# The head of a two-FFN attention kernel: constant matmuls ahead of the data, ternary weights by quarters, one block normalized on ScalarE

## The chip, the cores and the metric

The kernel runs on one core of a Trainium2 chip. The core has five engines that run side by side, each through its own instructions in order: TensorE (PE in the profile, PEld its weight loads), VectorE (DVE), ScalarE (ACT), GpSimd (POOL) and SyncE (SP, which here only issues transfers). They wait for each other through semaphores. The metric is the device time of one execution in microseconds, the median over several runs.

## The reference

The input x is 16 sequences of 256 tokens of 256 features, in fp32: 4096 rows of 256. Three stages each add to it:

```
x = x + 0.5 * ffn(layernorm(x))
x = x + attention(layernorm(x))          # 16 heads of 16, rotary, causal, softmax
x = x + 0.5 * ffn(layernorm(x))          # the same ffn weights

ffn(h) = gelu(h @ q(w1).T + b1) @ q(w2).T + b2
q(w)   = clip(round(w / mean(|w|)), -1, 1)
```

w1 is 1024 x 256 and w2 is 256 x 1024. So before the first FFN matmul can run, the mean of the absolute values of all of w1 has to be known, and before the second, that of w2. The rounded values are -1, 0 and 1: an element is 1 where it is over half the mean, and -1 where it is under minus half the mean.

## The kernel before

The rows are held in SBUF in 8 blocks of 512 tokens (`xs`), 4 groups of 128 partitions each. The two FFN stages run block by block; the attention stage runs sequence by sequence and is staggered with them. Only the head of the first FFN stage is touched here.

The order of the work on each engine is the order in which the program's lines issue it: the wrapper `InOrder` (lines 159 to 174) keeps every operation of an engine in program order. All these operations carry the wrapper's line, L167, in the profile, and are told apart by the tiles they write and read.

Loading. SP and ScalarE issue the transfers: block 0 of x, w1, b1, w2, b2, then the other seven blocks of x, then the attention weights. GpSimd meanwhile fills constants, among them `averaging` (128 x 128, line 119).

`begin` (line 352) does the head of the FFN. `measure` takes the layer-norm statistics of the block's four groups on VectorE (`stats`, two instructions for each group, line 178), and `finish_stats` turns four variances into reciprocal standard deviations (`rstd`) on GpSimd, in two instructions. `sizes` (line 208) sums the absolute values of a weight matrix, one part on VectorE and the rest on ScalarE for w1, both parts on ScalarE for w2. `prepare` normalizes the four groups (`xn`). `threshold` (line 221) lets TensorE sum over partitions by a matmul with `averaging`, and VectorE writes plus and minus half the mean (`half`). `signs` (line 232) makes the ternary values of a part of a matrix with two VectorE instructions: "smaller than minus half" into the result, then "greater than plus half, minus what is there". `turn_in` transposes one half of the normalized features with four TensorE transposes, ScalarE casts the result to the rounded matmul type (`xnT`, the high part), and VectorE subtracts to get the rest, so that a value goes through TensorE as a high part and a rest.

`step(u)` (line 366) is one of 64 steps and two late ones; i is the block and f one of 8 slices of 128 hidden features. In it `up` (line 301) does four matmuls of 512 columns into a PSUM tile `m` (2 buffers), ScalarE computes the gelu twice (`h_high`, rounded, and `h_whole`), and VectorE, or GpSimd for f = 1, 3, 5, subtracts (`h_rest`). `down` (line 322) does the eight matmuls of the slice two steps earlier with w2's ternary values (`w2q`). An up uses the slice f of w1's ternary values (`w1q`), a down the slice f of w2q.

In the first block the steps also carry, in this order after the up: threshold and signs of the first half of w2 at step 0, signs of the second half at step 3, statistics of block 1 at step 1, of block 2 at steps 4 to 7, the normalization of block 1 at step 3 on VectorE, its two turn_in at steps 5 and 6, and on GpSimd the halving of b2 at step 4 and its addition to x at step 6. Both halves of w1 are made in `begin`, one before and one after the transposes of block 0.

Of the kernel before, what the change touches and what calls it, by code (L numbers as in the profile page):

```python
# [8 lines left out]
FP = mybir.dt.float32  # L9
FR = mybir.dt.float32r  # L10
AF = mybir.ActivationFunctionType
ALU = mybir.AluOpType
# [17 lines left out]
def kernel(  # L30
# [144 lines left out]
    def tokens(n):  # L175
        return xs[n // BT][:, n % BT, :]
# [14 lines left out]
        )  # L191

    def normalize(ln, n, to, engine=None):
        (engine or vector).tensor_scalar(
            to,
            tokens(n),
            mv[ln][:, n, 0:1],
            rstd[ln][:, n : n + 1],
            ALU.subtract,
            ALU.mult,  # L200
        )
# [6 lines left out]
    def sizes(n):  # L208
        for k in range(2):
            part = (flat1, flat2)[n][:, k * FF : (k + 1) * FF]  # L210
            total = totals[n][:, k : k + 1]
            if n == 0 and k == 0:
                vector.tensor_reduce(total, part, AX.X, ALU.add, apply_absolute_value=True)
            else:

                size = w2q[:, k * NFC // 2 : (k + 1) * NFC // 2, :]
                scalar.activation(
                    size.rearrange("p k d -> p (k d)"), part, AF.Abs, accum_out=total
                )

    def threshold(n):
        mean = ps_mm.tile([P, 1], FP, name="mm")
# [9 lines left out]
    def signs(n, of):  # L232

        w, to = of((w1, w2)[n]), of((w1q, w2q)[n])
        vector.tensor_scalar(to, w, half[n][:, 1:2], None, ALU.is_lt)
        vector.scalar_tensor_tensor(
            to, w, half[n][:, 0:1], to.bitcast(FP), ALU.is_gt, ALU.subtract
        )
# [34 lines left out]
    def ffn(ln, after):  # L273
        xn, xnT, hT, ys = {}, {}, {}, {}

        def measure(i):
            if ln == 0:
                for t in range(BT):
                    stats(0, i * BT + t)
                finish_stats(0, i * BT, BT)  # L280
# [20 lines left out]
        def up(i, f):  # L301
            h = ps_m.tile([P, TB], FP, name="m")
            for n in range(2):
                for k in range(KC):
                    tensor.matmul(
                        h,
                        w1q[:, k, f * P : (f + 1) * P],
                        xnT[i][n][:, k, :],
                        start=(n == 0 and k == 0),
                        stop=(n == 1 and k == KC - 1),  # L310
                    )
            high = fp.tile([P, TB], FR, name="h_high", bufs=LATE + 3)
            rest = fp.tile([P, TB], FR, name="h_rest", bufs=LATE + 3)
            whole = fp.tile([P, TB], FP, name="h_whole", bufs=3)
            scalar.activation(high, h, AF.Gelu, bias=b1_sb[:, f : f + 1])
            scalar.activation(whole, h, AF.Gelu, bias=b1_sb[:, f : f + 1])

            engine = gpsimd if f in (1, 3, 5) and not (ln == 0 and i == NBLK - 1) else vector
            engine.tensor_sub(rest, whole, high.bitcast(FP))
            hT[i, f] = (high, rest)  # L320

        def down(i, f):
# [20 lines left out]
            if f == NFC - 1:  # L343
# [5 lines left out]
                for t in range(0, BT, 2):  # L349
                    after(i, t)  # L350

        def begin():
            measure(0)
            if ln == 0:
                sizes(0)
            prepare(0)
            if ln == 0:
                threshold(0)
                signs(0, lambda w: w[:, :, 0 : FF // 2])
            for k in range(KC):  # L360
                turn_in(0, k)()
            if ln == 0:
                signs(0, lambda w: w[:, :, FF // 2 :])
                sizes(1)

        def step(u):
            i, f = divmod(u, NFC)
            if i < NBLK:
                up(i, f)
                if ln == 0 and u == 0:  # L370
                    threshold(1)
                if ln == 0 and u in (0, 3):
                    part = slice(0, NFC // 2) if u == 0 else slice(NFC // 2, NFC)
                    signs(1, lambda w: w[:, part, :])
                if ln == 0 and u == 4:
                    gpsimd.tensor_scalar(b2_sb, b2_sb, 0.5, 0.0, ALU.mult, ALU.add)
                if u == 1:
                    measure(1)
                if ln == 0 and f >= 4 and i + 2 < NBLK:
                    stats(0, (i + 2) * BT + f - 4)  # L380
                    if f == NFC - 1:
                        finish_stats(0, (i + 2) * BT, BT)
                if i + 1 < NBLK:
                    if f == 3:
                        prepare(i + 1)
                    if f in (5, 6):
                        turn_in(i + 1, f - 5)()
                if f == (1 if i == NBLK - 1 else 6):
                    add_bias(i)
            if u >= LATE:  # L390
                down(*divmod(u - LATE, NFC))
            if ln == 0 and u == 2 * NFC + 2:
                make_tables()
            if ln == 0 and u < (NBLK - 1) * NFC and later:
                later.pop(0)()
# [425 lines left out]
```

## Time and profile before

| | us |
|---|---|
| median of 3 runs | 626.92 (625.38 to 626.99) |
| the profiled execution | 622.22 |
| its span | 620.4 |
| TensorE busy | 599.5 (97%) |
| VectorE busy | 461.2 (74%) |
| ScalarE busy | 416.3 (67%) |
| GpSimd busy | 300.9 (49%) |

The span is what the profiler saw from the first to the last instruction; the execution's own time lies 1.8 us above it. Busy time counts an engine's instructions; matmuls overlap, and their ends are modelled, so a busy TensorE may still be a slow one. In a timeline row the first number is the start in us from the span's start, the second the time that the merged instructions took from the first start to the last end; then the engine, the operation, the tiles written and read, shapes and count. "idle before" in square brackets names what ended the engine's wait. An fp32 matmul shows as two records, one in the rounded type as one. The engine table of the page reads, by slices of the span, that TensorE is busy nine tenths and more in all but the first slice and one later.

### The profile page before, as it was taken

What the parts mean: (1) busy time and instruction counts of PE and PEld (TensorE: products, weight loads), DVE (VectorE), ACT (ScalarE), POOL (GpSimd) and SP (SyncE); (2) the same over time, 40 slices, a digit from 0 to 9 for tenths busy, and PEclk for the clock granted to TensorE, in tenths of its full rate; (3) what the DMA queues carried; (4) which work ended last, traced back from release to release, by engine and by line L of the source; (5) the groups of instructions that cost most, each with busy time, mean ns of one, the idle gap of its engine ahead of it and who ended that gap; (6) DMA issues with size and microseconds to landing.
All of it is one profiled execution on the core that took longest, in us unless ns stands there. A gap on an engine that the chain in (4) does not pass through costs nothing.

```text
span 620.4 us, 14716 instructions
## 1 busy us (share of the span) xinstructions
PE 599.5 (97%) x5580; PEld 486.6 (78%) x5580; DVE 461.2 (74%) x1654; ACT 416.3 (67%) x716; POOL 300.9 (49%) x273
## 2 busy tenths in 40 slices
PE   4999999999999999999999999999998999999997
PEld 3798999887667777777777777777766798888886
DVE  6877777786788888888888888888886465555553
ACT  4666766664576677676777677767765676676674
POOL 3655555782464455545564456453430243334443
PEclk9999999999999999999999999999999999999999
DMA  8800000000001000100001000100100011011001
GB/s 285 180 22 1 2 1 18 17 1 18 20 35 38 19 21 36 38 27 29 19 36 38 20 20 36 37 20 21 36 4 2 1 35 35 34 35 35 27 21 55
DMA packets 25478, 21.30 MB, mean 34 GB/s; under 512 B 10944, under 2 KB 21056, under 8 KB 25408
## 3 DMA queue, kind: packets, MB, share of 16 engines
q1 hardware_dynamic: 24848, 19.44, 9.8%
q8 instruction: 44, 0.72, 0.5%
q10 hardware_dynamic: 560, 0.92, 0.4%
q14 instruction: 26, 0.21, 0.1%
HBM read 7.51 MB, written 4.19 MB: 19 GB/s over the span
## 4 chain that ended last, share of the span: by engine, by line
PE 89%; DVE 5%; ACT 3%; issue 1%; DMA 1%; POOL 1%; DVEq 0%; SPq 0%; POOLq 0%
PE mm L167 38%; PE w L167 29%; PE m L167 22%; DMA w<-in_w1T_dram 1%; DVE h_rest L167 1%; DVE xn L167 1%; ACT h_high L167 1%; ACT h_whole L167 1%; DVE w2q L167 1%; DVE st L167 1%; DVE w L167 0%; DVE x L167 0%; DVE masked L167 0%; DVE mv L167 0%; ACT pT L167 0%
## 5 line engine op out<-in xcount | busy, mean ns | idle before, releaser
L167 DVE CUSTOM_DVE_ANT_0 masked<-m,mask_q 128x128 f32<-128x128 f32 x480 | 142.7, 354 | 41.0 <-PE m L167 39.7
L167 PE MATMUL m<-xnT,w1q 128*128 128x512 f32 x512 | 145.1, 404 | 0.8 <-ACT xnT L167 0.7
L167 ACT ACTIVATE h_high<-m,b_sb 128x512 fp32r<-128x512 f32 x128 | 88.5, 691 | 78.2 <-PE m L167 78.1
L167 DVE TENSOR_TENSOR h_rest<-h_whole,h_high 128x512 fp32r<-128x512 f32 x83 | 75.0, 904 | 72.0 <-ACT h_whole L167 71.5
L167 ACT ACTIVATE pT<-w 128x768 f32<-128x768 f32 x128 | 104.1, 815 | 31.4 <-DVE w L167 24.9
L167 PE MATMUL w<-qT,kT 32*128 32x256 f32 (+1 forms) x1024 | 120.6, 348 | 1.9 <-ACT pT L167 1.8
L167 PE MATMUL w<-w2q,h_high 128*128 128x256 f32 x480 | 120.8, 285 | 0.7 <-DVE w2q L167 0.7
L167 PE MATMUL w<-w2q,h_rest 128*128 128x256 f32 x480 | 117.8, 279 | 0.4 <-POOL h_rest L167 0.3
L167 PEld LDWEIGHTS w<-qT,kT 32*128 32x128 f32 x1024 | 89.9, 184 | 33.0 <-issue 25.9
L167 PE MATMUL m<-kT,qT 32*128 32x128 f32 x960 | 114.9, 349 | 0.7 <-ACT kT L167 0.7
L167 POOL TENSOR_TENSOR h_rest<-h_whole,h_high 128x512 fp32r<-128x512 f32 x45 | 60.1, 1335 | 108.5 <-ACT h_whole L167 108.4
L167 PEld LDWEIGHTS m<-xnT,w1q 128*128 128x128 f32 x512 | 88.3, 190 | 16.7 <-DVE xnT L167 2.9
L167 PEld LDWEIGHTS w<-w2q,h_rest 128*128 128x128 f32 x480 | 90.4, 188 | 5.1 <-POOL h_rest L167 0.7
L167 PEld LDWEIGHTS w<-w2q,h_high 128*128 128x128 f32 x480 | 90.3, 188 | 5.2 <-DVE w2q L167 1.2
L167 DVE TENSOR_TENSOR w<-w,mask_k 128x512 f32<-128x512 f32 x128 | 88.8, 695 | 7.1 <-PE w L167 7.0
L167 ACT ACTIVATE h_whole<-m,b_sb 128x512 f32<-128x512 f32 x128 | 87.3, 682 | 0.0
L167 PEld LDWEIGHTS m<-kT,qT 32*128 32x128 f32 x960 | 65.9, 185 | 2.9 <-ACT kT L167 1.6
L167 POOL TENSOR_TENSOR w<-w,cosT 128x512 f32<-128x512 f32 x32 | 41.3, 1292 | 51.8 <-ACT w L167 31.9
L167 PE MATMUL mm<-xnT_a,wqk 128*128 128x256 f32 x256 | 62.2, 386 | 0.0
L167 POOL TENSOR_SCALAR var<-mv 128x4 f32<-128x4 f32 (+1 forms) x32 | 6.9, 216 | 106.2 <-DVE mv L167 105.6
L167 POOL TENSOR_TENSOR w<-w,sinT 128x512 f32<-128x512 f32 x32 | 41.0, 1280 | 26.0 <-DMA w<-w 25.9
L167 PEld LDWEIGHTS mm<-xnT_a,wqk 128*128 128x128 f32 x256 | 46.1, 190 | 7.6 <-issue 0.7
(86 smaller groups left out, 918.9 us busy)
## 6 DMA issues: line engine op xcount, KB each, us to landing
w<-w SPq DMA_DIRECT2D x64, 128.0 KB
out_dram<-x SPq DMA_DIRECT2D x15, 256.0 KB
x<-in_x_dram SPq DMA_DIRECT2D x7, 512.0 KB
w<-in_w2T_dram SPq DMA_DIRECT2D x1, 1024.0 KB
qT<-mT SPq DMA_DIRECT2D x64, 4.0 KB
w<-in_w1T_dram SPq DMA_DIRECT2D x1, 512.0 KB
w<-in_w1T_dram ACTq DMA_DIRECT2D x1, 512.0 KB
wqk<-in_wqkvT_dram SPq DMA_DIRECT2D x16, 32.0 KB
```

The costliest lines, as they stand in the source:

```text
L167: return tc.keep_in_program_order(getattr(self.engine, name)(*args, **kwargs))
```

## The change

Three things are changed, all in the head of the first FFN stage.

- `turn_on(n)` issues n matmuls of the constant tile with itself into a PSUM tile that nobody reads: 20 after the statistics of block 0 are issued, before TensorE's threshold of w1, and 4 after the transposes of block 0.
- The ternary values are made by quarters (two slices f of a matrix), not by halves. Quarter 0 of w1 comes before the transposes of block 0, quarter 1 after them; quarters 2 and 3 at steps 2 and 3. The threshold and quarter 0 of w2 are issued within `up` of step 0, between its gelu and its subtraction; quarter 1 at step 1, quarters 2 and 3 at steps 4 and 5.
- Block 1: its statistics are taken one group a step at steps 1 to 4, instead of all four at step 1, and finished at step 4. Its normalization goes from VectorE at step 3 to ScalarE at step 5, as `rstd * x - mean * rstd`; VectorE prepares the product `less` in one 128 x 1 instruction for each group. Its turn_in move from steps 5 and 6 to steps 6 and 7.

```diff
     def normalize(ln, n, to, engine=None):
+        if engine is scalar:
+            less = small.tile([P, 1], FP, name="less")
+            vector.scalar_tensor_tensor(
+                less, mv[ln][:, n, 0:1], -1.0, rstd[ln][:, n : n + 1], ALU.mult, ALU.mult
+            )
+            scalar.activation(
+                to, tokens(n), AF.Identity, bias=less, scale=rstd[ln][:, n : n + 1]
+            )
+            return
...
+    def turn_on(n):
+
+        on = ps_m.tile([P, P], FP, name="m")
+        for _ in range(n):
+            tensor.matmul(on, averaging, averaging, start=True, stop=True)
...
             scalar.activation(whole, h, AF.Gelu, bias=b1_sb[:, f : f + 1])
+            if ln == 0 and (i, f) == (0, 0):
+                threshold(1)
+                signs(1, quarter(1, 0))
...
+        def quarter(n, k):
+
+            at = slice(2 * k * P, 2 * (k + 1) * P) if n == 0 else slice(2 * k, 2 * (k + 1))
+            return (lambda w: w[:, :, at]) if n == 0 else (lambda w: w[:, at, :])
+
         def begin():
             measure(0)
             if ln == 0:
+                turn_on(20)
                 sizes(0)
             prepare(0)
             if ln == 0:
                 threshold(0)
-                signs(0, lambda w: w[:, :, 0 : FF // 2])
+                signs(0, quarter(0, 0))
             for k in range(KC):
                 turn_in(0, k)()
             if ln == 0:
-                signs(0, lambda w: w[:, :, FF // 2 :])
+                turn_on(4)
+                signs(0, quarter(0, 1))
                 sizes(1)
...
                 up(i, f)
-                if ln == 0 and u == 0:
-                    threshold(1)
-                if ln == 0 and u in (0, 3):
-                    part = slice(0, NFC // 2) if u == 0 else slice(NFC // 2, NFC)
-                    signs(1, lambda w: w[:, part, :])
+
+                soon = {1: (1, 1), 2: (0, 2), 3: (0, 3), 4: (1, 2), 5: (1, 3)}
+                if ln == 0 and u in soon:
+                    signs(soon[u][0], quarter(*soon[u]))
                 if ln == 0 and u == 4:
                     gpsimd.tensor_scalar(b2_sb, b2_sb, 0.5, 0.0, ALU.mult, ALU.add)
-                if u == 1:
-                    measure(1)
+                if ln == 0 and 1 <= u <= BT:
+                    stats(0, BT + u - 1)
+                    if u == BT:
+                        finish_stats(0, BT, BT)
...
-                    if f == 3:
-                        prepare(i + 1)
-                    if f in (5, 6):
-                        turn_in(i + 1, f - 5)()
+
+                    late = 2 if ln == 0 and i == 0 else 0
+                    if f == 3 + late:
+                        prepare(i + 1, scalar if late else None)
+                    if f in (5 + late // 2, 6 + late // 2):
+                        turn_in(i + 1, f - 5 - late // 2)()
```

## The prediction

> **What bounds the kernel now.** First the page: its chain that ended last says which engine sets the end.
>
> ```profile
> PE 89%; DVE 5%; ACT 3%; issue 1%; DMA 1%; POOL 1%; DVEq 0%; SPq 0%; POOLq 0%
> ```
>
> TensorE (PE) sets it, so a change is worth what it moves PE. All edits lie before the second block's first matmul, so second I read PE's timeline there.
>
> ```profile
> 8.22 0.98 PE L167 MATMUL mm<-totals,averaging 128*128 128x1 f32 x4 [8.22 <-DVE totals L167]
> 11.75 2.05 PE L167 MATMUL m<-xnT,w1q 128*128 128x512 f32 x4 [0.74 <-ACT xnT L167]
> 14.30 3.08 PE L167 MATMUL m<-xnT,w1q 128*128 128x512 f32 x8
> ...
> 27.30 0.60 PE L167 MATMUL mm<-ident,xn 128*128 128x128 f32 x4
> 27.65 0.36 PE L167 MATMUL w<-w2q,h_high 128*128 128x256 f32 x1
> ...
> 28.67 1.09 PE L167 MATMUL m<-xnT,w1q 128*128 128x512 f32 x4
> 29.60 0.28 PE L167 MATMUL w<-w2q,h_high 128*128 128x256 f32 x1
> ...
> 30.54 1.09 PE L167 MATMUL m<-xnT,w1q 128*128 128x512 f32 x4
> 31.47 0.28 PE L167 MATMUL w<-w2q,h_high 128*128 128x256 f32 x1
> ```
>
> From 27.65 on there is no gap: an up is 0.93 us (28.67 to 29.60), a down 0.94 (29.60 to 30.54), four transposes 0.35 (27.30 to 27.65). The second block starts at 30.54 and its first up is over at 31.47. From 11.75 the same work without gaps (8 ups, 6 downs, 2 x 4 transposes) would take 13.8 us, not 18.8: 5.0 us of slow matmuls and waits are there to be won. At full speed an up ends 1.09 after its start and ScalarE follows at 1.13; the ups at 11.75 and 14.30 took nearly twice that, though the granted clock in the rows of all windows is 1.00.
>
> Third, what the other engines did there (VectorE is DVE, GpSimd POOL):
>
> ```profile
> 9.53 0.75 DVE L167 TENSOR_SCALAR w1q<-w,half 128x1024 fp32r<-128x1024 f32 x1
> 10.32 1.28 DVE L167 SCALAR_TENSOR_TENSOR w1q<-w,half,w1q 128x1024 fp32r<-128x1024 f32 x1
> 11.52 1.28 DVE L167 TENSOR_TENSOR xnT<-mm,xnT 128x512 fp32r<-128x512 f32 x2
> ...
> 15.74 0.22 DVE L167 TENSOR_SCALAR half<-mm 128x1 f32<-128x1 f32 x2
> ...
> 21.49 1.28 DVE L167 SCALAR_TENSOR_TENSOR w2q<-w,half,w2q 128x1024 fp32r<-128x1024 f32 x1
> 22.69 2.52 DVE L167 TENSOR_SCALAR xn<-x,mv,rstd 128x256 f32<-128x256 f32 x4
> 25.13 0.68 DVE L167 TENSOR_TENSOR h_rest<-h_whole,h_high 128x512 fp32r<-128x512 f32 x1
> ```
> ```profile
> 22.29 1.64 POOL L167 TENSOR_TENSOR h_rest<-h_whole,h_high 128x512 fp32r<-128x512 f32 x1
> ```
> ```profile
> L167 ACT ACTIVATE kT<-w,one,own 128x256 f32<-128x256 f32 x64 | 38.1, 595 | 0.0
> ```
>
> DVE hardly rests from 8 to 27 us: it is the limit of this stretch. And DVE and POOL get in each other's way: the four normalizations at 22.69 took 2.52 us, against 1.37 for the same four at 7.99, because POOL's subtraction of 22.29 ran to 23.93 first; PE's first transpose of them starts at 24.23.
>
> **The change, part by part.** *Quarters.* A half costs 0.79 + 1.20 from start to start (9.53, 10.32, 11.52). A quarter's first instruction lies between the 256-wide normalization (0.32) and 0.75: by the line through them 0.48, 0.52 to the dependent next. The second costs like a 512-wide subtraction, 0.61 start to start. A quarter is 1.14, eight cost 9.1 against 8.0 for four halves: +1.1 us on DVE. Ends: 1.00 (half a half) and 1.22 (0.08 more).
>
> *The second block.* Its four DVE normalizations (2.5 us) go. ScalarE gets four of the kind of the kT row (per-partition scale and bias): 0.49 apart, 2.0 in all (ends: 0.40, the qT row's distance, and 0.59, kT's own duration), all of it on the path, since ScalarE is in order behind the sixth gelu pair and in front of the seventh. DVE gets four 128x1 instructions, 0.07 to 0.11 each as for the halves' thresholds: 0.3. They wait for rstd, with DVE's step-6 subtraction queued behind them, ScalarE's seventh gelu pair and both casts behind the normalizations, and on PE all downs from the fifth on behind the transposes. And rstd for the fourth statistic, which moves from behind the first w2 half to between the third w2 quarter and the next block's statistic. Transposes move one step later (steps 6 and 7), so only a down and one up stand between the last ones and the second block.
>
> *The 24 constant matmuls.* An fp32 matmul shows as two records. Cold, a record is 0.21 (the transposes at 9.06) to 0.245 (four in 0.98); warm, 0.09 (transposes) to 0.12 (half of a 256-wide fp32 record, 0.24). The first 20 can start at 1.1, after POOL's memset of the constants, and must be over by 8.22. All 40 records cold end at 9.6 to 10.9; warm from the start at 4.7 to 5.9. PE went fast at about 16.5 after an unbroken run from 13.17, 3.4 us: so I take 15 cold and 25 warm records, end at 7.6, cost nothing; the cover is the wait for the first weights, and beyond it every us delays the threshold and all of DVE's chain. The later four fill about 9.9 to 10.85, where the first up waits for weights anyway.
>
> *The new order, followed.* Threshold 9.27 as before (DVE's own normalizations end there). First quarter to 10.67, two subtractions to 11.89, second quarter to 13.03. PE, fast, has the transposes done at 9.9, ScalarE's casts end 10.97 (before 11.63), its two size sums 13.15 (before 13.72), so the w2 threshold reaches DVE at 13.55 instead of 15.74. That is the gain: 2.2 us. From there DVE must do, before the four small instructions: thresholds 0.25, six quarters 6.84, three subtractions 1.83, six statistics of 0.56 (4 of this block, 2 of the next), 3.36: together 12.3 us. Before, the same place needed 15.74 to 25.2 for thresholds, two halves, one subtraction, four statistics and the normalizations.
>
> Without any wait, the small instructions start at 25.85 and the normalized block is ready at 28.1, three microseconds later than the 25.2 of before. Two waits come on top. POOL's subtraction of step 1 becomes due at 16.05, among quarters, and that of step 3 at about 19.0; each holds DVE for 1.17 (such a row of POOL, 38.61 to 40.04, begins to work at 38.87, when DVE's third of four normalizations from 37.86 is over by 0.34 each), less what DVE can do meanwhile: statistics run beside POOL unhurt (0.39 to 0.42 at 17.98 to 20.0). And the subtraction of step 4 waits 0.3 for its gelu, since its up needs the third w1 quarter. With both POOL turns in full the third w1 quarter is ready at 21.35 (fifth up 21.45, before 21.04), the fourth statistic at 26.2, rstd at 27.5, hidden behind DVE's last quarter; small instructions 28.46, xn ready 30.5, transposes over at T = 30.65. If POOL's turns fall partly beside statistics, T = 29.25.
>
> From T: down 0.94, up 0.93, ScalarE's gelu pair ends at T + 3.25, cast T + 3.83; DVE in order does a subtraction (from T + 3.4), a statistic, then the transposed rest to T + 5.2; PE's first up of block two ends at T + 5.6. Before, 31.47. So T = 30.65 gives +4.8, T = 29.25 gives +3.4, no POOL wait (T = 28.2) +2.3. The unseen prices add ends of -1.2 (6 x 0.14 and 0.36) and +0.9 (6 x 0.08 and 0.4). I take +4.8: POOL asks within 0.05 us of the end of a DVE instruction, and in the row of 22.29 the waiting POOL went first.
>
> *Hidden edits.* The constants' results are read by nobody, so their buffers hold up only PE itself. SP's queue and its DMAs are unchanged; the second block's x is read from about 17 instead of 17.98, and the 3.1 MB up to its end are moved by about 12 (the windows of 2 us from 2 to 12 show 302, 404, 360, 278 and 214 GB/s). GpSimd's halving of b2 now runs before the rstd pair and costs 0.4 of POOL, idle then. Without that idleness it would delay rstd by 0.4. After 31.47 PE is without gaps and everything follows by the same shift.
>
> The sum: the profiled execution took 622.22 (span 620.4), so 622.2 + 4.8 = 627.0; the median of the runs shown is 626.92, 4.7 above that execution, and I carry the shift over: **631.7 us**.
>
> A rule that speaks against the change: the Trainium skill, "TensorE: Matmul & The Clock Gate", section "HAM oscillation — how this bites in real kernels", warns of idle gaps over about 3.4 us, after which the array falls back to half clock. By that page alone the sum would be an estimated 1.7 us higher (half of one 3.4 us window). No row here shows PE falling back.
>
> **Rivals.**
> 1. *PE goes slow again.* With T = 30.65 PE's seventh up ends at 26.1, and PE sits 4.4 us. For: the slow ups at the start. Against: no gap that long exists later in this trace. Bounds: nothing, to one down, two ups and transposes at half speed, 0.94 + 2 x 0.92 + 0.5 = 3.3. Total +6.5 as a middle, +8.1 at most: 633.4 to 635.0.
> 2. *The first 20 run too long.* All cold ends at 9.6 to 10.9, 1.4 to 2.7 behind 8.22: +6.2 to +7.5, 633.1 to 634.4. Against: the 3.4 us of 13.17 to 16.5.
> 3. *POOL finds its turns beside statistics.* +2.3, 629.2; decided by whether its two subtractions start inside statistics.
> 4. *Faster.* DVE's chain of 12.3 us is cheaper. Break-even needs T = 25.9, so small instructions at 23.6: 10.1 us without any POOL wait, that is quarters at 0.77 instead of 1.14. Below that the gain of the early threshold survives, 0.6 us for each 0.1; at 0.40 it is -2.1, 624.8. Against: the instruction rows above; a fixed part of 0.2 per instruction is not halved.
> 5. *No effect:* a longer wait at the second block but shorter ones behind it. For this PE would need gaps just behind 31.47; it has none to 40.
>
> **How the numbers follow.** The forecast, +3.4 to +4.8, 0.52; rival 1, 0.20; rival 2, 0.08; rival 3, 0.09 (half of it slower by over 0.3%, as 2.3 us is 0.37%); rival 4, 0.06 (all counted as faster); rival 5, 0.05. 0.3%, about 1.9 us, is what a measurement can tell from no change. Slower 0.52 + 0.20 + 0.08 + 0.05 = 0.85, same 0.04 + 0.05 = 0.09, faster 0.06. The range runs from just under rival 3 to rival 1's upper part: 628.8 to 634.8, which leaves out rivals 4 and 5 and the extremes of 1 and 2.
>
> **What would show it.** Right: fast first ups (about 1.1 us, not 2.05); w2's threshold on DVE near 13.5; quarter pairs near 1.14; POOL's subtractions between quarters; the ScalarE normalizations starting near 28.5; a PE gap of about 4 us before the transposes; second block's first up over near 36. Wrong: those normalizations starting before 24, or the 20 matmuls ending after 8.3.

## The result and the profile after

The changed kernel takes 634.59 us (median of 6 runs, 631.73 to 637.81), the kernel before 626.75 (6 runs, 622.22 to 626.99): 7.8 us more. The ratio on record is 1.0167, 95% interval 1.0138 to 1.0195; that is more than the quotient of these two medians (1.0125), and how it was formed is not recorded. Of 626.75 it is 10.5 us. The kernel is slower, as forecast, but by 7.8 to 10.5 us instead of 4.8. The profiled execution took 634.47 us (span 632.7). Some profiled executions have stretches of half TensorE clock late in the kernel (after 150 us) and some have none; of the other executions only the mean granted clock is known, and the lower it is, the longer they took. Before's profiled execution, without any such stretch, took 622.2; after's shortest run, whose granted clock of 0.995 is what the head's stretches alone give (6.8 us at half clock, read below, are 0.5% of 632), took 631.73. So at an equal late clock the change costs 9.5 us, and that is what has to be explained.

The page of after first, its chain that ended last:

```profile
PE 87%; DVE 6%; ACT 3%; issue 1%; POOL 1%; DVEq 0%; POOLq 0%
```

PE's share fell from 89 to 87%, DVE's rose. Then PE's timeline from the start to the second block (start, duration, instruction, the wait before it in brackets):

```profile
11.01 1.61 PE L167 MATMUL m<-xnT,w1q 128*128 128x512 f32 x4
...
13.30 2.11 PE L167 MATMUL m<-xnT,w1q 128*128 128x512 f32 x8
...
21.12 1.17 PE L167 MATMUL m<-xnT,w1q 128*128 128x512 f32 x4 [2.43 <-DVE w1q L167]
...
23.46 1.91 PE L167 MATMUL m<-xnT,w1q 128*128 128x512 f32 x4
...
29.57 0.33 PE L167 MATMUL mm<-ident,xn 128*128 128x128 f32 x1 [2.00 <-ACT xn L167]
...
31.88 0.33 PE L167 MATMUL mm<-ident,xn 128*128 128x128 f32 x1 [1.48 <-ACT xn L167]
...
32.45 0.36 PE L167 MATMUL w<-w2q,h_high 128*128 128x256 f32 x1
...
34.01 1.91 PE L167 MATMUL m<-xnT,w1q 128*128 128x512 f32 x4
...
39.13 0.50 PE L167 MATMUL m<-xnT,w1q 128*128 128x512 f32 x1 [0.65 <-DVE xnT L167]
39.47 0.28 PE L167 MATMUL w<-w2q,h_high 128*128 128x256 f32 x1
```

The early ups are faster, as meant: the first takes 1.61 us, against 2.05, the next two 2.11 together, against 3.08. The fifth up waits 2.43 us for its quarter of w1. The down behind the transposes, forecast at T = 30.65, starts at 32.45. And the second block's first up, over at 31.47 before, is over at 39.47 (call this time the mark): +8.0 us, of which the forecast had 4.8. Two ups, at 23.46 and 34.01, take 1.91 instead of 1.09.

DVE's and POOL's timelines tell why:

```profile
13.48 0.22 DVE L167 TENSOR_SCALAR half<-mm 128x1 f32<-128x1 f32 x2 [0.24 <-PE mm L167]
13.80 0.49 DVE L167 TENSOR_SCALAR w2q<-w,half 128x512 fp32r<-128x512 f32 x1
14.32 0.75 DVE L167 SCALAR_TENSOR_TENSOR w2q<-w,half,w2q 128x512 fp32r<-128x512 f32 x1
...
19.35 1.63 DVE L167 SCALAR_TENSOR_TENSOR w1q<-w,half,w1q 128x512 fp32r<-128x512 f32 x1
...
28.22 3.04 DVE L167 SCALAR_TENSOR_TENSOR less<-mv,rstd 128x1 f32<-128x1 f32 x4
```
```profile
19.12 1.30 POOL L167 TENSOR_TENSOR h_rest<-h_whole,h_high 128x512 fp32r<-128x512 f32 x1 [1.90 <-ACT h_whole L167]
...
28.83 2.34 POOL L167 TENSOR_TENSOR x<-x,b_sb 128x1024 f32<-128x1024 f32 x1
```

w2's threshold comes at 13.48, a quarter's second instruction takes 0.75 and 1.63 beside POOL's subtraction, the four small instructions start at 28.22: all close to the forecast. But these four, 128x1 each, take 3.04 us, across POOL's addition of b2 (28.83 to 31.17). ScalarE's timeline shows the same break, two normalizations before the end of that addition and two after it:

```profile
28.92 1.09 ACT L167 ACTIVATE xn<-x,less,rstd 128x256 f32<-128x256 f32 x2 [2.25 <-DVE less L167]
31.23 1.09 ACT L167 ACTIVATE xn<-x,less,rstd 128x256 f32<-128x256 f32 x2 [1.21 <-DVE less L167]
```

And the table of windows shows the clock (window, its length, busy time of PE, PEld, DVE, ACT, POOL, then the granted PE clock):

```profile
20.00:22.00 2.00, 0.88 (x4) 0.77 (x5) 1.93 (x5) 0.00 (x0) 1.16 (x2) 1.00 1.17 315
22.00:24.00 2.00, 2.00 (x12) 1.86 (x11) 1.58 (x4) 1.27 (x2) 0.00 (x0) 0.64 0.71 71
24.00:26.00 2.00, 2.00 (x8) 1.71 (x7) 1.93 (x6) 0.59 (x2) 0.00 (x0) 0.50 0.37 38
...
32.00:34.00 2.00, 1.84 (x10) 1.65 (x11) 0.50 (x1) 1.94 (x4) 0.00 (x0) 0.70 0.56 143
34.00:36.00 2.00, 2.00 (x7) 1.51 (x7) 1.28 (x4) 0.04 (x1) 0.00 (x0) 0.50 0.00 0
```

PE fell to half clock twice: (1 - 0.64) x 2 x 2 = 1.4 us of the window from 22 and all 2.0 of the next, 3.4 us; the same again from about 32.8. (Near the start such rows read 1.00 although PE is slow there: the 40 records of constants from 1.12 on take 6.81 us, while 32 of the same kind take 3.73 in the run below that keeps the clock. The rows show a fall, not the slow beginning.) Each stretch follows a time in which PE had little to do.

### The profile page after: what moved, and what is told of

The parts are those of the page before. It is cut to its first block, busy times and chain, and to the rows that moved or that the text cites. A ratio compares the mean times of both kernels' runs of the same rounds, so it can differ in the third digit from the quotient of the medians.

```text
span 632.7 us, 14827 instructions
## 1 busy us (share of the span) xinstructions
PE 613.3 (97%) x5628; PEld 497.8 (79%) x5628; DVE 464.5 (73%) x1662; ACT 417.6 (66%) x720; POOL 299.9 (47%) x273
## 4 chain that ended last, share of the span: by engine, by line
PE 87%; DVE 6%; ACT 3%; issue 1%; POOL 1%; DVEq 0%; POOLq 0%
PE mm L167 37%; PE w L167 28%; PE m L167 22%; DVE h_rest L167 1%; DVE w2q L167 1%; ACT h_high L167 1%; ACT h_whole L167 1%; DVE st L167 1%; DVE xn L167 1%; DVE less L167 0%; DVE w L167 0%; DVE x L167 0%; DVE masked L167 0%; DVE w1q L167 0%; DVE mv L167 0%
## 5 line engine op out<-in xcount | busy, mean ns | idle before, releaser
L167 PE MATMUL w<-w2q,h_high 128*128 128x256 f32 x480 | 123.0, 288 | 0.0
L167 PE MATMUL w<-w2q,h_rest 128*128 128x256 f32 x480 | 120.8, 284 | 0.5 <-POOL h_rest L167 0.2
L167 PEld LDWEIGHTS w<-w2q,h_high 128*128 128x128 f32 x480 | 91.7, 191 | 4.4 <-issue 0.3
```

Of the source, the lines that this page charges most:

```text
L167: return tc.keep_in_program_order(getattr(self.engine, name)(*args, **kwargs))
```

## The experiments

The theory at the start (A): the head is longer because the second block's statistics and normalization now stand behind all of DVE's quarters; on top come what POOL holds up and the half clock. The rivals: it is the quarters, the constants, or the ScalarE normalization as such, in whatever place.

### The three parts alone

**Constants only** (before, with the constants):

```diff
             if ln == 0:
+                turn_on(20)
                 sizes(0)
...
             if ln == 0:
+                turn_on(4)
                 signs(0, lambda w: w[:, :, FF // 2 :])
```

> The kernel before with the 24 constant matmuls alone. Mark: the end of the second block's first up, 31.47 us in the kernel before, 39.47 in the changed one. Theory A (VectorE's chain sets the head, the changed kernel is late because of the order of VectorE's work): the first ups are fast, but the first down still waits for the w2 half that VectorE finishes near 18.1, so the mark stays at 31.5 (within 0.3) and the time is the same. Theory C (TensorE's clock is what matters): the mark comes 1 to 2 us earlier.

Measured: 625.15 us against 624.7, ratio 1.0007 (0.9976 to 1.0038). PE's first ups are fast, and the time goes to the wait behind them. PE stood still all of 16 to 18 in the profiled execution, and then fell to half clock (the table of windows of this run):

```profile
16.00:18.00 2.00, 0.00 (x0) 0.00 (x0) 1.96 (x2) 1.25 (x3) 1.32 (x1) 1.00 1.10 347
18.00:20.00 2.00, 1.39 (x9) 1.39 (x10) 1.90 (x7) 0.00 (x0) 0.00 (x0) 0.82 1.11 350
20.00:22.00 2.00, 2.00 (x7) 1.61 (x7) 1.93 (x6) 0.10 (x1) 1.13 (x2) 0.50 1.16 323
```

The mark was at 33.14, 1.6 us behind the 31.5 that A expected; half of 3.4 us at half clock is 1.7. C, which expected it 1 to 2 us earlier, does not hold. The runs at a granted clock of 1.000 took 622.6 to 622.7, 0.2 to 0.6 more than before's at 0.998 to 1.000 beside them (622.1 to 622.4): alone the constants give nothing.

**Quarters only** (before, with the quarters and their places):

```diff
-                signs(0, lambda w: w[:, :, 0 : FF // 2])
+                signs(0, quarter(0, 0))
...
+                soon = {1: (1, 1), 2: (0, 2), 3: (0, 3), 4: (1, 2), 5: (1, 3)}
+                if ln == 0 and u in soon:
+                    signs(soon[u][0], quarter(*soon[u]))
```

> The kernel before with the quarters alone, in the changed kernel's order; second block as before (statistics at step 1, VectorE normalization at step 3), no constants. A: 1.1 us more VectorE work, and w1's last two quarters now stand ahead of the normalization: mark near 33 (+1.5). Theory B (what costs is the second block's new place and engine, the quarters are free): mark 31.5.

Measured: 626.84 us, ratio 1.0049 (1.0026 to 1.0072), mark 34.70, 1.7 us behind what A expected. The fifth up waits 3.11 us for its quarter, and 3.4 us of half clock follow here too. So in this order the quarters are not free.

**Second block only** (before, with its later statistics, its ScalarE normalization and its later transposes):

```diff
-                if u == 1:
-                    measure(1)
+                if ln == 0 and 1 <= u <= BT:
+                    stats(0, BT + u - 1)
+                    if u == BT:
+                        finish_stats(0, BT, BT)
...
+                    late = 2 if ln == 0 and i == 0 else 0
+                    if f == 3 + late:
+                        prepare(i + 1, scalar if late else None)
```

> The kernel before with the second block's edits alone (one statistic a step, ScalarE normalization at step 5, turn-in at steps 6 and 7), halves, no constants. A: rstd comes after the fourth statistic at about 25 to 26, GpSimd's addition of b2 may hold the four small instructions for 2 us: mark 35 to 37 (+4 to +5.5). B: the whole of the +8.0, mark 39 or later.

Measured: 630.37 us, ratio 1.011 (1.0072 to 1.0149), mark 38.35, between what A and B expected: this part alone puts the mark 6.9 us back. PE waits from 26.0 to 28.1 and again for 1.34 us before the third transpose, because POOL's addition (2.35 us) cuts the four small instructions in two here as well (3.58 us for the four). The windows from 28 to 34 have a clock of 0.50. The three marks (+1.7, +3.2 and +6.9) do not add up to the +8.0: each part alone draws half clock of its own.

### Is it the addition of b2, is it the clock?

**Bias late** (the changed kernel, the first block's addition of b2 two steps later):

```diff
-                if f == (1 if i == NBLK - 1 else 6):
+                if f == (1 if i == NBLK - 1 else 6) and not (ln == 0 and i == 0):
                     add_bias(i)
+                if ln == 0 and u == NFC:
+                    add_bias(0)
```

> The changed kernel with GpSimd's addition of b2 to block 0 moved from step 6 to step 8. A: the four small instructions take 0.3 us instead of 3.04, the normalized block comes 1.9 us earlier, mark 37.5 or, if TensorE then also keeps its clock, 36. B: it is the late rstd alone, mark stays at 39.5.

Measured once: 630.91 us. The small instructions take 0.88 us instead of 3.04, DVE's timeline:

```profile
29.09 0.88 DVE L167 SCALAR_TENSOR_TENSOR less<-mv,rstd 128x1 f32<-128x1 f32 x4
```

That the addition held them is shown. The mark still came at 39.03, for in this execution the first half clock fell on the fifth up itself (1.96 us from 21.22) and put everything behind it 0.9 us back; the second began at about 31.6.

**Clock kept** (the changed kernel, with more constants in PE's two gaps):

```diff
             if i < NBLK:
+                if ln == 0 and u == 4:
+                    turn_on(8)
                 up(i, f)
+                if ln == 0 and u == 6:
+                    turn_on(16)
```

> The changed kernel with 8 more constant matmuls ahead of the fifth up and 16 ahead of the second block's first transposes, where TensorE stood idle for 2.4 and about 5 us. C (the two half-clock stretches of 3.4 us that follow those gaps cost what they slow, 1.7 us each, 3.4 together): mark 36. A with the clock as a smaller part (the first stretch lies ahead of a wait and costs little; of the second, the down and the up ahead of the gelu pair count, 0.5 + 0.9): mark 38.0.

Measured: 630.26 us, ratio 1.0086 (1.0052 to 1.0119); the granted clock is 1.00 in every window of the head, the mark at 38.23. Beside the changed kernel's 39.47 that is 1.2 us, what A expected of a clock that is the smaller part (38.0), and not C's 36. The mark, here and in the next run:

```profile
38.23 0.28 PE L167 MATMUL w<-w2q,h_high 128*128 128x256 f32 x1
```

**Both** (the two edits together):

> The kept-clock kernel with GpSimd's addition of b2 to block 0 at step 8 as well. A: the four small instructions at about 28.2 take 0.3 to 0.9 us, 2 us less than with the addition beside them: mark 36.0 to 36.3. B (the late rstd alone): no gain over the kept clock, 38.

```profile
37.02 0.28 PE L167 MATMUL w<-w2q,h_high 128*128 128x256 f32 x1
```

Measured once: 633.66 us, with 10.2 us of late half clock; the mark at 37.02, the earliest so far with the change's own order, and 0.7 to 1.0 behind what was expected. The clock is 1.00 in every window of the head here too. So with the clock kept, moving the addition is worth 1.2 us of the mark.

### Is it the order?

**Second block early** (the changed kernel with statistics, normalization and transposes in the steps where before has them; quarters, constants and ScalarE stay):

```diff
-                if ln == 0 and 1 <= u <= BT:
-                    stats(0, BT + u - 1)
...
+                if u == 1:
+                    measure(1)
...
-                    late = 2 if ln == 0 and i == 0 else 0
+                    late = 0
```

> The changed kernel with the second block back at its old steps (statistics all at step 1, normalization at step 3, turn-in at 5 and 6) but still on ScalarE; quarters and constants stay. A: the small instructions stand ahead of both late w2 quarters, about 23.7, the normalized block is ready at 26, mark 32.5 to 34 (+1 to +2.5 on the kernel before, -6 on the changed one). B with ScalarE, not the place, as the cause: mark 37 or later.

Measured: 632.35 us, ratio 1.0113 (1.0075 to 1.0151), mark 36.55. The expectation was missed by 2.5 us: the four statistics in one piece put the third w1 quarter back (the fifth up waits 3.10 us), 6.8 us of half clock follow, and POOL's addition now stretches a w2 quarter from 0.75 to 2.78 us. The old places alone take 2.9 us off the mark, and not 6.

**New order** (the second block's statistics in one piece at step 1; the third w1 quarter before the second w2 quarter; normalization after the fourth up, transposes at steps 5 and 6; one POOL subtraction on DVE; addition of b2 late; two of these edits are shown):

```diff
+                if ln == 0 and u == 3:
+                    prepare(1, scalar)
-                soon = {1: (1, 1), 2: (0, 2), 3: (0, 3), 4: (1, 2), 5: (1, 3)}
+                soon = {1: (0, 2), 2: (1, 1), 3: (0, 3), 4: (1, 2), 5: (1, 3)}
...
```

> A new order out of the findings: constants and quarters stay; the second block's four statistics stand right behind the first subtraction, beside GpSimd's one, then w1's third quarter, then w2's second; VectorE does the subtraction of step 3; the ScalarE normalization is at step 3, turn-in at 5 and 6; the addition of b2 to block 0 is at step 8. A: third w1 quarter ready at 19.1 instead of 20.9, small instructions at 21 to 22 and not held up, normalized block at 23.5 to 24, TensorE without a gap over 1 us: mark 29.7 (-1.8 on the kernel before, 0.3% faster). B and C: no better than 31.5.

Measured: 627.03 us, ratio 1.004 (1.0016 to 1.0064), mark 32.03, clock 1.00 in the whole head. With another order and the addition late, 7.4 of the head's 8.0 us are gone; the expected mark of 29.7 was missed by 2.3, and the head is not shorter than before's. What was left is a wait of PE at the very end of the head, for DVE's transposed rest:

```profile
31.69 0.50 PE L167 MATMUL m<-xnT,w1q 128*128 128x512 f32 x1 [1.23 <-DVE xnT L167]
```

With a mark only 0.6 behind that of before, the kernel was still 1 to 2 us slower at a granted clock of 1.000 (624.1 to 624.4 against 622.2 to 623.2): something outside the head costs time too.

### Something outside the head: addresses

Behind the head the changed kernel's blocks take longer. PE's timelines of before, of after and, further down, of a run yet to be told: the first ups of the fifth and the sixth block of the first stage, and for before the first down between them.

```profile
79.03 1.09 PE L167 MATMUL m<-xnT,w1q 128*128 128x512 f32 x4
79.96 0.28 PE L167 MATMUL w<-w2q,h_high 128*128 128x256 f32 x1
...
80.90 1.09 PE L167 MATMUL m<-xnT,w1q 128*128 128x512 f32 x4
...
94.85 1.09 PE L167 MATMUL m<-xnT,w1q 128*128 128x512 f32 x4
```
```profile
87.40 1.09 PE L167 MATMUL m<-xnT,w1q 128*128 128x512 f32 x4
...
103.37 1.09 PE L167 MATMUL m<-xnT,w1q 128*128 128x512 f32 x4
```

Before, 15.82 us; after, 15.97. In the third stage it is 16.08 against 16.19. No instruction of the change is there. But the built program places the new tile `less` (four buffers of 32 bytes) in a pool ahead of others, so that the transposed and hidden activations that PE reads (xnT, h_high, h_rest) and more stand 128 bytes higher in each partition than before. The quantized weights do not move.

**`less` elsewhere** (the changed kernel, `less` from a pool of its own at the end):

```diff
+    lp = ctx.enter_context(tc.tile_pool(name="lessp", bufs=4))
...
-            less = small.tile([P, 1], FP, name="less")
+            less = lp.tile([P, 1], FP, name="less")
```

> The changed kernel with the four small tiles `less` taken from a pool of their own at the end, so that every other tile stands at the address that it has in the kernel before (in the changed kernel all that follow them stand 128 bytes higher). No instruction is added or moved. Theory P (placement): the blocks of the first stage behind the head go back from 15.97 us to 15.81 and those of the third from 16.19 to 16.08, which is 7 x 0.16 + 8 x 0.11 = 2.0 us: about 632.6 us. Theory Q (the slower blocks follow from how the head ran, or from the ScalarE normalization itself): 15.97 and 16.19 stay, 634.6 us. Either way the second block's first up ends near 39.5, as in the changed kernel.

Measured: 635.89 us, ratio 1.0152 (1.0123 to 1.0181), so the total was missed; but its head drew more half clock than the changed kernel's (windows from 34 to 38 at 0.50 and 0.52, mark 40.79). The blocks are back: ups at 88.39 and 104.20 stand one block apart, 15.81, and the third stage's take 16.08. At a granted clock of 0.988 its one run took 632.88 us, the changed kernel's two 634.34 and 634.70.

**Four pads** (before, with four unused tiles of 32 bytes in that pool, written once by GpSimd during the loads):

```diff
     nc.gpsimd.memset(power, -0.5)
+    for _ in range(4):
+        pad = small.tile([P, 1], FP, name="pad")
+        nc.gpsimd.memset(pad, 0.0)
```

> The kernel before with four unused tiles of 32 bytes in the same pool, written once by GpSimd while everything loads: the addresses of all later tiles go up by the same 128 bytes, and nothing else of the change is in it. Theory P (placement): the head as before (mark 31.5), then blocks of 15.97 us in the first stage and 16.19 in the third, about 2 us slower (628.7 us, ratio 1.003). Theory Q: 15.81 and 16.08, no difference (626.7).

```profile
79.49 1.09 PE L170 MATMUL m<-xnT,w1q 128*128 128x512 f32 x4
80.42 0.28 PE L170 MATMUL w<-w2q,h_high 128*128 128x256 f32 x1
...
81.38 1.09 PE L170 MATMUL m<-xnT,w1q 128*128 128x512 f32 x4
...
95.46 0.87 PE L170 MATMUL m<-xnT,w1q 128*128 128x512 f32 x3
```

15.97 us, and 16.19 in the third stage, with nothing of the change in the kernel and a mark of 31.60. The medians (625.40 against 624.86, ratio 1.0009, 0.9984 to 1.0035) hide it behind the late half clock; the runs at a granted clock of 1.000 took 623.69 to 623.75, before's beside them (0.998 to 1.000) 622.22 to 622.35 and one 623.06: +1.4 us against the first three. Placement it is. The expected 2.0 was too much: farther on, where other matmuls stand between the ups, eight of them take no longer (115.46 to 132.68 before, 17.22; 116.12 to 133.31 here, 17.19).

**Other shifts** (2, 8, 16 and 6 pads: 64, 256, 512 and 192 bytes).

> The kernel before with two unused tiles of 32 bytes, so that later tiles stand 64 bytes higher. Read from it is only the length of a block: before 15.81 us (first stage) and 16.08 (third), at 128 bytes 15.97 and 16.19. If any departure from the old addresses costs, or the cost grows with the shift, 15.85 to 15.97 and 16.10 to 16.19. If the pace depends on the address within 256 bytes, any value from 15.7 to 16.0 is possible here, but not at 256.

> The same with eight tiles, 256 bytes. If the pace depends on the address within 256 bytes: 15.81 and 16.08, as before. If it depends on the address within 512 bytes or more, or on any departure: 15.9 or more, or another value.

> The same with sixteen tiles, 512 bytes. If the pace depends on the address within 256 or 512 bytes: 15.81 and 16.08. If on a longer period or on the distance between operands: another value.

> The kernel before with six unused tiles, so that later tiles stand 192 bytes higher. Blocks so far: 15.81 us at 0, 15.9 at 64, 15.97 at 128, 15.81 at 256 and 512 bytes. If the pace falls off and comes back evenly within 256 bytes, 15.87 to 15.92 here; if the old address is merely the best that was tried, less than 15.8 is possible.

The same block of the first stage, from the same rows of PE's timelines:

| shift, bytes | 0 | 64 | 128 | 192 | 256 | 512 |
|---|---|---|---|---|---|---|
| ups at | 79.03, 94.85 | 79.59, 95.49 | 79.49, 95.46 | 79.44, 95.32 | 79.18, 95.00 | 79.29, 95.11 |
| block, us | 15.82 | 15.90 | 15.97 | 15.88 | 15.82 | 15.82 |

One execution each is enough for a length that repeats block after block (total times 623.40, 626.96, 626.82 and 628.20 us, the last three with 10.2 us of late half clock). At these six shifts the pace goes with the address within 256 bytes and is worst half of that away from where the tiles stand in the kernel before. In the same rows the eight ups of the block take 7.47 us at shift 0 and 7.48 at 128, its eight downs 7.64 and 7.78 (the downs at 64 and 192: 7.74 and 7.78; at 256 and 512: 7.64 and 7.65). So the loss lies in the downs, which read h_high and h_rest, and not in the ups, although xnT moved by as much. In a down these two are loaded as weights and w2q, which did not move, is streamed; in an up xnT is streamed. Which of the two tiles does it, and by what mechanism, was not taken apart.

### All three losses taken away

**Three mended** (the changed kernel with its order kept; `less` elsewhere, bias late, clock kept):

> The changed kernel with the three extra losses taken away together: `less` in the pool of its own (old addresses), the first block's bias addition two steps later (so that it no longer holds the small instructions), and 24 constants more on PE in its two gaps (full clock). What is left should be the late statistics and the normalization behind them, the forecast's +4.8 us alone and what the constants themselves take: mark at 36.3 to 37.2, no half clock in the head, blocks of 15.81 and 16.08, and a run that has no half clock later either takes 5 to 5.7 us more than before's runs without one (622.2): 627.2 to 627.9 us. If there is a fourth loss, the blocks or the mark come out above that.

Measured: 631.10 us, ratio 1.0104 (1.0061 to 1.0146). The mark is at 36.95, the clock 1.00 throughout the head, the blocks 15.82 and 16.08; the one run at a granted clock of 1.000 took 627.57, 5.3 more than before's such runs. All three numbers are inside what was expected: no fourth loss shows. Against the run that only keeps the clock (630.02 to 630.36 at 1.000) that is 2.5 to 2.8 us, the 1.3 of the mark and the 1.4 of the blocks. What is left is the forecast's own +4.8 and a little more: DVE's timeline still has 0.88 us for the four small instructions, overlapped by POOL's third subtraction (from 27.56, 1.47 us), where the forecast had 0.3. PE's and DVE's timelines:

```profile
31.30 0.36 PE L168 MATMUL w<-w2q,h_high 128*128 128x256 f32 x1
...
36.95 0.28 PE L168 MATMUL w<-w2q,h_high 128*128 128x256 f32 x1
```
```profile
28.37 0.88 DVE L168 SCALAR_TENSOR_TENSOR less<-mv,rstd 128x1 f32<-128x1 f32 x4
```

### The parts in another order

**New order, second** (`less` elsewhere and computed after the fourth up; ScalarE's normalization behind the fifth up's gelu pair; both transposes at the start of step 6; the third block's statistics in steps 8 and 9; two POOL subtractions on DVE):

```diff
+                if ln == 0 and u == 4:
...
+                        shifted(0, BT + t, xn[1][:, t, :], lesses[t])
+                if ln == 0 and u == 6:
+                    todo = [turn_in(1, 0), turn_in(1, 1)]
...
+                if ln == 0 and u == 3:
+                    lesses.extend(shift(0, BT + t) for t in range(BT))
```

> All parts of the change in another order: constants, quarters in the order of need, the second block's statistics after the second up, its small instructions on VectorE at the end of the fourth step (before any GpSimd addition), its ScalarE normalization behind the fifth step's gelu pair, both transposes at the start of the seventh step, the third block's statistics two steps later, GpSimd's bias addition two steps later, GpSimd's second and third subtraction of the first block on VectorE, and `less` in the pool of its own. If what cost the change its gain is order alone, PE has no gap over 2 us after the first up, no half clock in the head, the mark falls at 29.0 to 29.7 and the kernel takes 1.8 to 2.5 us less than before (ratio 0.996 to 0.997), with blocks of 15.81 and 16.08. If the head is bound by the sum of VectorE's work (quarters, statistics, normalization) in any order, the mark stays at or above 31.5 and the ratio is 1.000 or more.

Measured: 625.86 us, ratio 1.0007 (0.9983 to 1.0030), mark 33.03, not the 29.0 to 29.7 that order alone was expected to give. The bias addition was placed two steps later, but POOL, which had lost its subtractions, had nothing in front of it and started it at once. DVE's and POOL's timelines:

```profile
21.48 2.63 DVE L168 TENSOR_SCALAR w1q<-w,half 128x512 fp32r<-128x512 f32 x1
```
```profile
21.10 2.72 POOL L168 TENSOR_TENSOR x<-x,b_sb 128x1024 f32<-128x1024 f32 x1
```

The fourth w1 quarter lost 2.1 us, the small instructions came at 24.81, PE waited and fell to half clock at about 27. By this run alone it could still be the sum of DVE's work that bounds the head in any order; the next run decides.

**New order, third** (the same, POOL keeps its third subtraction; the last two w2 quarters together):

```diff
-            engine = gpsimd if f in (1, 3, 5) and not (ln == 0 and (i == NBLK - 1 or i == 0 and f in (3, 5))) else vector
+            engine = gpsimd if f in (1, 3, 5) and not (ln == 0 and (i == NBLK - 1 or i == 0 and f == 3)) else vector
...
-                soon = {1: (0, 2), 2: (1, 1), 3: (0, 3), 4: (1, 2), 5: (1, 3)}
+                soon = {1: [(0, 2)], 2: [(1, 1)], 3: [(0, 3)], 4: [(1, 2), (1, 3)]}
```

> As the second new order, with two things mended that its trace shows: GpSimd keeps the third subtraction (h of the sixth up), so that its bias addition can start only behind it, at about 28, and not at 21.1, where it stretched the fourth w1 quarter's first instruction from 0.49 to 2.63 us; and the last two w2 quarters stand together after the fifth up. If the 2.1 us of that quarter were what kept the mark at 33.0, it falls to 29.5 to 30.5, PE is without a gap over 2 us, and the kernel takes 1 to 2 us less than before (ratio 0.997 to 0.998). If VectorE is the bound of the head in any order, or the bias addition only finds the next instruction to stretch, the mark stays at 31.5 to 33 and the ratio is 1.000 to 1.002.

DVE's and PE's timelines:

```profile
21.48 0.47 DVE L168 TENSOR_SCALAR w1q<-w,half 128x512 fp32r<-128x512 f32 x1
22.00 0.75 DVE L168 SCALAR_TENSOR_TENSOR w1q<-w,half,w1q 128x512 fp32r<-128x512 f32 x1
22.66 0.36 DVE L168 SCALAR_TENSOR_TENSOR less<-mv,rstd 128x1 f32<-128x1 f32 x4
```
```profile
24.66 1.09 PE L168 MATMUL mm<-ident,xn 128*128 128x128 f32 x8
25.51 0.36 PE L168 MATMUL w<-w2q,h_high 128*128 128x256 f32 x1
...
28.46 1.31 PE L168 MATMUL m<-xnT,w1q 128*128 128x512 f32 x4
29.61 0.28 PE L168 MATMUL w<-w2q,h_high 128*128 128x256 f32 x1
```

The quarter takes 0.47 + 0.75 again, the four small instructions 0.36, the eight transposes run without a wait, and the mark is at 29.61, 1.9 us earlier than before and inside what was expected. So the sum of DVE's work does not hold the head at 31.5 in any order, and with the quarters, the constants and ScalarE's normalization all in it the head can be shorter than before's. The median is 623.91 us against 624.00, ratio 0.9979 (0.9952 to 1.0006): by that interval alone no gain is shown, because late half clock spreads both kernels over 5 us. Sorted by granted clock the two kernels do not overlap: at 0.998 to 1.000 the new order takes 620.01 to 620.24 (4 runs) and before 622.14 to 622.83 (6); at 0.990 it takes 624.67 to 625.12 (6) and before 626.76 to 627.12 (4). That is 2.0 to 2.1 us, as much as the mark and a little more. It is the one version here that is ahead of both kernels. It holds more than a new order (a POOL subtraction on DVE, the third block's statistics later); which of these edits brings how much was not taken apart.

## Why the prediction was right in direction and wrong by half

The direction and the mechanism of the one term in the sum held. The forecast failed in what it left at nothing: POOL's hold on the four small instructions, the half clock, and the blocks behind the head. The difference of 9.5 us adds up, but for 0.2:

| term | forecast, us | measured, us | shown by |
|---|---|---|---|
| late statistics and normalization in the head | 4.8 | 4.9 | what is left with the three losses taken away: mark 36.95 - 31.47 = 5.5, less the 0.6 of the next row |
| small instructions held by POOL's third subtraction | 0 | 0.6 | three mended: 0.88 instead of the forecast's 0.3 |
| small instructions held by the b2 addition | 0 | 1.2 | clock kept against both: mark 38.23 to 37.02 |
| half clock in the head | 0 (rival 1) | 1.2 | clock kept: mark 39.47 to 38.23 |
| slower blocks behind the head | 0 | 1.4 | four pads: 623.7 against 622.3 |
| sum | 4.8 | 9.3 | 631.73 - 622.22 = 9.5 |

The two rows on the small instructions together are 1.8, as much as the down behind the transposes came late (32.45 against T = 30.65). That the first row comes from DVE's list is read from its timeline, where it has hardly a gap from 13.48 to 28.22; no run takes the late statistics alone away. And that the changed kernel's 634.59 lies inside the range of 628.8 to 634.8 is luck: the upper part of that range was meant for rivals 1 and 2, of which 2 did not happen and 1 makes 1.2 of the 9.5.

Step by step:

- *Constants end at 7.6, cost nothing.* They ended at 7.93 and delayed nothing. (The 3.4 us behind that price were counted from 13.17; PE's rows of before have no wait from 11.75 on, so the run before PE got fast was longer.) That they bring nothing by themselves (ratio 1.0007) fits the forecast, in which DVE set the head.
- *w2's threshold at 13.55.* 13.48. The gain of 2.2 us is real and lies at the wrong end of DVE's chain.
- *A quarter pair is 1.14.* 0.52 + 0.67 = 1.19 from start to start (13.80, 14.32, 14.99).
- *POOL's subtractions hold DVE among quarters.* Both did, by 0.9 us each instead of 1.17 (1.67 and 1.63 instead of 0.75); the fifth up was forecast at 21.45 and came at 21.12, the small instructions at 28.46 and came at 28.22.
- *DVE gets four 128x1 instructions, 0.3 in all; xn ready 30.5.* This step failed. They were priced by their size. The forecast applied POOL's hold to the quarters and did not look at what POOL does at 28.2: its own list of POOL's work had the halving of b2 and not the addition of 2.4 us, which before's trace shows from 26.93 on (the row below). With it and the third subtraction the four took 3.04 instead of 0.3, and T came at 32.45 instead of 30.65. The Trainium skill, "SBUF — State Buffer", section "Who interferes with whom", says that a VectorE instruction with two SBUF inputs contends with a GpSimd instruction that reads SBUF; the row of 3.04 us agrees, at a size of one element per partition.

```profile
26.93 2.41 POOL L167 TENSOR_TENSOR x<-x,b_sb 128x1024 f32<-128x1024 f32 x1
```

- *From T the mark follows in 5.6.* It did where the clock was kept (31.30 to 36.95 with three mended); in the changed kernel it took 7.0.
- *Rival 1, PE goes slow again, +6.5 to +8.1, chance 0.20.* This step of the sum failed: it happened, in addition to the forecast, and with T at 32.45 instead of 30.65 the mark landed at +8.0. The sum left it at nothing although the forecast itself had PE sit 4.4 us ahead of the transposes. PE fell there, and before that after 2.43 us of waiting (21.12), and in the run with the bias late after 2.41. The Trainium skill, "TensorE: Matmul & The Clock Gate", section "HAM oscillation — how this bites in real kernels", warns of gaps over about 3.4 us; these rows fell sooner.
- *After 31.47 PE is without gaps and everything follows by the same shift.* This step failed too. There were no gaps, yet the blocks of the first and the third stage read above took 0.16 and 0.11 us more, through four tiles of 32 bytes.
- *The shift is carried over to the median.* Its form is right, but both medians are drawn from runs that differ by up to 5 us with the granted clock; the difference of the medians (7.8) and that at an equal clock (9.5) are not the same number.
- *Rival 4, faster only if quarters cost 0.77 or less.* Too narrow: it held the order fixed. With the order changed and quarters at 1.19 the third new order gains 2 us.

## What to carry to other kernels

When a small instruction is moved onto an engine that another one can hold up, as POOL did DVE here, look up what the other engine does at the new time, not only at the old one: here the price was set by that other instruction and not by its own size. Work taken off a crowded engine is worth nothing when the piece that others wait for is queued behind the rest; order the engine's list by who waits, and only then divide it finer. And when a change adds even one tiny tile, compare the addresses of the tiles that PE reads before believing a loss of a per cent in stages that the change does not touch.

## What the runs showed of the hardware

- The pace of this dense chain of matmuls went with where the tiles h_high and h_rest, and those that moved with them, stand within 256 bytes of a partition: 15.82 us a block at shifts of 0, 256 and 512 bytes, 15.90 and 15.88 at 64 and 192, 15.97 at 128.
- A half clock in the head mostly followed PE waits of 2.0 to 3.1 us and lasted 3.4 or 6.8 us. The second new order fell with a wait of 1.16 us and a window in which PE was busy 0.96 of 2 us (24 to 26). The first new order did not, with a wait of 1.23 us and a window in which PE was busy 0.77 of 2 us (30 to 32), nor did the third, whose waits stayed under 0.6. So neither the longest wait nor the busy share of such a window alone decides; what does is not shown. Filling the gaps with constants kept the clock in the profiled executions of all three runs with that edit.
- Executions of one kernel differ by up to 5 us, and the time goes with the granted clock (before, in 17 runs beside the third new order: 622.1 to 622.8 at 0.998 to 1.000, 624.0 to 624.7 at 0.996, 626.8 to 627.1 at 0.990). In the profiles the late stretches of half clock lie mostly around the change from the second stage to the third, where before's PE is busy 0.90 of 2 us (472 to 474); whether filling such waits would remove them was not tried. The clock row of the page of the run with three losses mended, in 40 slices of 15.8 us, shows such a stretch between 473 and 504 us:

```profile
PEclk9999999999999999999999999999997899999999
```

- POOL's addition over 128x1024 held a 128x1 DVE instruction for over 2 us (3.04 to 0.88 for the four without it), and a 128x512 one for 2.2 (2.63 instead of 0.47).
